# Stages of short products in a new order, mixing in 64x32 parts, and a new count of idle TensorE instructions

## The chip, the cores and the metric

The kernel runs on one core of a Trainium2 chip. The metric is device time in microseconds of one execution; the median of three runs is 1237.55 us (1237.3 to 1237.75). All arithmetic is in float32.

## What is computed

The input x has 128 sequences of 32 tokens with 512 channels. One layer does this (cut to what matters, norms and shapes in words):

```python
# x: (128, 32, 512); cond, adapter: one index per sequence
c = einsum('bct,bcd->bdt', x, cond_w[cond])          # mixing: a 32x32 matrix per sequence, over its tokens
q, k, v = split(clip(c @ w_qkv.T, -8, 8))            # projections; q and k then go through a layer norm
s = einsum('bqhd,bkhd->bhqk', q, k) / 4 + bias       # scores: 32 heads of 16, causal, ALiBi
x = x + einsum('bhqk,bkhd->bqhd', softmax(s), v) @ w_out.T      # weighted values, output projection
h = einsum('bsi,boi->bso', x, adapt_w[adapter])      # adapters: a 512x512 matrix per sequence
y = relu(h @ up_w) ** 2 @ down_w                     # shared part
y = y + (h @ fc1.T @ expert.T) * sum(top2(h @ gate_w)) @ fc2    # routed part, three matrices folded into one
out = x + layernorm(y)
```

## The kernel before

The 4096 tokens are cut into 32 tiles of 128 rows, so a tile is four sequences. Two tiles are a pair, whose shared part is computed together.

After a prologue for the first tiles, a loop runs over periods t = 2, 3, and so on. One period works on several tiles at once: weighted values, output projection and the turning of x for tile t; adapters for t-1; scores and softmax for t+1; mixing, q/k/v projections and the turning of q and k for t+2; routing for t-2; and half of the shared part of a pair. Even periods hold the up products (pu), odd ones the down products (pd), cut into eight parts `fill(0)` to `fill(7)` that stand between the other steps. TensorE's order is that of the program, with some orders fixed by hand: `after` orders two instructions without a wait on the chip, `wait` makes one wait for another. A planner in the framework orders the other engines' instructions by their dependencies and its own costs.

The order of TensorE in a period is: weighted values (`weigh`, psum po, L484), adapters (`adapt`, pad, L536), scores (`scores`, psc, L414), first half of the router (`route`, pr, L555), mixing (`mix`, pxc, L290), fill(0), two projections (`project`, pqkv, L307), output projection (`attend`, pw, L506), fills 1 to 3, third projection, second half of the router, fills 4 to 7.

A float32 product runs as two passes, each a weight load and a product. The full-size products use the whole array (128 rows x 128 columns). The adapters and weighted values use 128x32 parts of it, four side by side, each with its own 32 output rows; the scores use 64x32 parts, eight side by side, in two PSUM banks, one for each half of the rows. Mixing uses the whole array: its moving operand `blk` is a 128x128 matrix with the four sequences' 32x32 matrices on its diagonal (made by GpSimd in `blend`), its weights are the four 128-column parts of x. ScalarE copies the result to xcT (L295).

The scores' inputs are made late in the period before: q and k go to HBM and back to be turned (`swap`), ScalarE scales them (`scale`, L386 and L400), and VectorE spreads k over the heads (kx, L390). ScalarE's relu of the up products is L585.

`fill_up` puts idle instructions (`nc.tensor.nop`, L99) behind a fill: 7 in even periods, 71 in odd ones, 116 in period 2, spread over the eight fills. The next product that goes through `product` is ordered behind them.

`load_adapters` issues the next tile's adapter weights (4 MB) on SP's queue; in the loop its first transfer waits for the row maxima `mx` of tile t+1 (`cue`). PSUM has eight banks, handed out in turn.

Of the kernel before, what the change touches and what calls it, by code (L numbers as in the profile page):

```python
# [34 lines left out]
ROUT = (0, NE + D // 2, NE + D)  # L35


SHORT = (7, 71)
FIRST = 116
CLIP = 8.0  # L40
EPS = 1e-5
NEG = -1.0e30
# [3 lines left out]
def adaln_attn_ffn(  # L46
# [45 lines left out]


    queue = []

    def fill_up(n):

        for _ in range(n):
            nop = nc.tensor.nop("fill")  # L99
            after(nop, queue[-1])  # L100
            queue[:] = [nop]

    def product(*args, **kwargs):
        ins = nc.tensor.matmul(*args, **kwargs)  # L104
        if queue:
            after(ins, queue.pop())
        return ins


# [175 lines left out]
    def mix(t):  # L285

        s = tiles[t]
        pxc = bank(f"pxc_{t}")
        for c in range(DC):
            nc.tensor.matmul(  # L290
                pxc[:, ts(c, P)], lhsT=s["x"][:, ts(c, P)],
                rhs=s["blk"].rearrange("p a b -> p (a b)"), start=True, stop=True,
            )
        s["xcT"] = w2.tile([P, DC, P], F32, tag="xcT", name=f"xcT_{t}")
        nc.scalar.copy(s["xcT"].rearrange("p c n -> p (c n)"), pxc)  # L295

    def project(t, i, chunks=range(DC)):

        s = tiles[t]
        if chunks[0] == 0:  # L300
            if i == 0:
                s["qk"] = w2.tile([P, 2, D], F32, tag="qk", name=f"qk_{t}")
                s["v"] = w2.tile([P, D], F32, tag="v", name=f"v_{t}")
                s["mv"] = sm.tile([P, 2, 2], F32, tag="mv2", name=f"mv_{t}")
            s["pp", i] = bank(f"pqkv_{t}_{i}")
        for c in chunks:
            nc.tensor.matmul(  # L307
                s["pp", i], lhsT=s["xcT"][:, c, :], rhs=wqkv_sb[:, c, ts(i, D)],
                start=(c == 0), stop=(c == DC - 1),
            )  # L310
        if chunks[-1] < DC - 1:
            return
        nc.vector.tensor_scalar(  # L313
            out=s["qk"][:, i, :] if i < 2 else s["v"], in0=s["pp", i],
            scalar1=-CLIP, scalar2=CLIP, op0=ALU.max, op1=ALU.min,
        )
        if i < 2:
            st = sm.tile([P, 6], F32, tag="st", name=f"st_{t}_{i}")
            s["stats"] = nc.vector.bn_stats(out=st, in_=s["qk"][:, i, :])
            nc.vector.bn_aggr(out=s["mv"][:, i, :], in_=st)  # L320
# [13 lines left out]
                    after(add, done)  # L334

    last_flip = []
    last_pad = []

    def swap(srcs, name):

# [38 lines left out]
    def scale(t):  # L379

        s = tiles[t]
        q, k = s["T"][:, :, 0], s["T"][:, :, 1]

        s["kx"] = w1.tile([P, DC, SEQ, HQ, S], F32, tag="kx", name=f"kx_{t}")
        for c in range(DC):
            nc.scalar.activation(  # L386
                k[:, :, c], s["raw"][1][:, :, c], AF.Identity,
                bias=lnc[:, 3, c : c + 1], scale=lnc[:, 2, c : c + 1],
            )
            kx = nc.vector.tensor_tensor(  # L390
                out=s["kx"][:, c],
                in0=k[:, :, c].unsqueeze(2).broadcast_to([P, SEQ, HQ, S]),
                in1=m_half.unsqueeze(1).unsqueeze(3).broadcast_to([P, SEQ, HQ, S]),
                op=ALU.mult,
            )

            if c == 0 and last_flip:
                after(kx, last_flip[-1])
        for c in range(DC):
            nc.scalar.activation(  # L400
                q[:, :, c], s["raw"][0][:, :, c], AF.Identity,
                bias=qaff[:, 1, c : c + 1], scale=qaff[:, 0, c : c + 1],
            )

    def scores(t):

        s = tiles[t]
        s["s"] = w1.tile([P, H, S], F32, tag="s", name=f"s_{t}")
        banks = [bank(f"psc_{t}_{r}") for r in range(2)]
        for c in range(DC):  # L410
            for b in range(SEQ):
                for r in range(2):
                    rows_r = slice(r * P // 2, (r + 1) * P // 2)
                    psc = nc.tensor.matmul(  # L414
                        banks[r][ts(b, S), ts(c, HQ * S)],
                        lhsT=s["T"][rows_r, b, 0, c],
                        rhs=s["kx"][rows_r, c, b].rearrange("p h k -> p (h k)"),
                        start=True, stop=True,
                    )
                    if last_pad:  # L420
                        after(psc, last_pad.pop())
        s["psc"] = psc
        for r in range(2):
            add = nc.vector.tensor_tensor(
                out=s["s"].rearrange("p (c r h) k -> p r c (h k)", c=DC, r=2)[:, r],
                in0=banks[r].rearrange("p (c n) -> p c n", c=DC),
                in1=bias_sb.rearrange("p (c r n) -> p r c n", c=DC, r=2)[:, r],
                op=ALU.add,
            )
            s.setdefault("adds", []).append(add)  # L430
# [12 lines left out]
    def share(t):  # L443
        s = tiles[t]
        den = sm.tile([P, H], F32, tag="den", name=f"den_{t}")
        nc.vector.tensor_reduce(out=den, in_=s["s"], axis=AX.X, op=ALU.add)  # L446
        rden = sm.tile([P, H], F32, tag="rden", name=f"rden_{t}")
        nc.vector.reciprocal(rden, den)  # L448
        nc.gpsimd.tensor_tensor(  # L449
            out=s["s"], in0=s["s"], in1=rden.unsqueeze(2).broadcast_to([P, H, S]), op=ALU.mult  # L450
        )
# [28 lines left out]
    def weigh(t):  # L480
        s = tiles[t]
        po = bank(f"po_{t}")
        for h in range(H):
            nc.tensor.matmul(  # L484
                po[ts(h % 4, S), :].rearrange(
                    "p (e b i d) -> p e i b d", e=DC, b=SEQ, d=HD
                )[:, h // 8, h // 4 % 2],
                lhsT=s["pT"][:, h, :],
                rhs=s["vx"][h // (H // 2)][:, h % (H // 2)],
                start=True, stop=True,  # L490
            )


        s["aT"] = w1.tile([P, DC, SEQ, S], F32, tag="aT", name=f"aT_{t}")
        aT = nc.vector.transpose(
            out=s["aT"].rearrange("p e b q -> p (e b q)"), in_=po
        )
        if t == 0:
            after(tiles[2]["stats"], aT)

    def attend(t):

        s = tiles[t]
        pw = bank(f"pw_{t}")
        for g in range(4):
            nc.tensor.matmul(  # L506
                pw, lhsT=s["aT"][:, g].rearrange("p b q -> p (b q)"), rhs=wout_sb[:, g, :],
                start=(g == 0), stop=(g == 3),
            )
        nc.vector.tensor_tensor(out=s["x"], in0=s["x"], in1=pw, op=ALU.add)  # L510

    def turn_x(t):
# [9 lines left out]
    def adapt(t):  # L522
# [10 lines left out]
        for j in range(SEQ):  # L533
            for c in range(DC):
                for g in range(DC):
                    last_pad[:] = [nc.tensor.matmul(  # L536
                        pad[ts(g, S), ts(j, P)], lhsT=s["xT"][:, j, c],
                        rhs=s["adw"][c // 2][j][:, c % 2, ts(g, P)],
                        start=(c == 0), stop=(c == DC - 1),
                    )]  # L540
        nc.vector.transpose(
            out=pairs[t // GRP]["hT"][:, :, ts(t % GRP, P)].rearrange(
                "p e (j n) -> p e j n", j=SEQ
            ),
            in_=pad.rearrange("p (j e d) -> p e j d", j=SEQ, d=S),
        )

    def route(t, half):

# [25 lines left out]
    def up(g, f):  # L575
# [6 lines left out]
                start=(c == 0), stop=(c == DC - 1),  # L582
            )
        a = hp.tile([P, GRP * P], F32, tag="act", name=f"act_{g}_{f}")
        nc.scalar.activation(a, pu[:, : GRP * P], AF.Relu)  # L585
        nc.gpsimd.tensor_tensor(out=a, in0=a, in1=a, op=ALU.mult)  # L586
        pair["acts"].append(a)
        return last
# [186 lines left out]
    for t in range(GRP, NTILE + GRP):  # L775
# [2 lines left out]

        def fill(i):
            last = up(g, i) if t % GRP == 0 else down(g * GRP + i // 4, i % 4)  # L780
            short = FIRST if t == GRP else SHORT[t % GRP]
            queue[:] = [last]
            fill_up(short // 8 + (i < short % 8))

        when(here and t > GRP, weigh, t)
        when(t <= NTILE, adapt, t - 1)
        when(ahead, scores, t + 1)
        when(ahead, exponent, t + 1)
        if here:


            load_adapters(t, tiles[t + 1]["mx"] if ahead else None)
        if t == GRP:
            after(
                nc.sync.dma_start(out=gam_sb, in_=gamma.broadcast_to([P, D])),
# [2 lines left out]
        when(t + 3 < NTILE, load, t + 3)  # L798
        when(t > GRP and t % GRP == 0, finish, t - GRP - 1)
        when(t > GRP, route, t - GRP, 0)  # L800
        when(two, mix, t + 2)
        fill(0)
        when(two, project, t + 2, 0)
        when(ahead, share, t + 1)
        when(two, project, t + 2, 1)
        when(ahead, flip, t + 1)
        when(two, normalise, t + 2)
        when(two, turn, t + 2)
        when(here, attend, t)
        when(here, turn_x, t)  # L810
        fill(1)
        fill(2)
# [91 lines left out]
```

## Time and profile before

| | |
|---|---|
| median of three runs | 1237.55 us (1237.3 to 1237.75) |
| the profiled execution | 1237.27 us, span 1235.5 us |
| granted TensorE clock, mean | 0.999 |
| TensorE products (PE) | 1227.2 us busy, 99% |
| weight loads (PEld) | 790.5 us, 64% |
| VectorE, ScalarE, GpSimd | 658.3, 327.6, 431.5 us |
| one even and one odd period (from 607.06 us) | 37.77 and 37.69 us |

PE stands for the products of TensorE, PEld for its weight loads, PEldq for its sequencer's own instructions (semaphores, idle ones); DVE is VectorE, ACT ScalarE, POOL GpSimd, SP the engine that issues most transfers. A busy time is the union of the instructions' times; a product's recorded time holds its way through the array, so products overlap in the records, and a stage's length is read from the chain of waits, which cuts the time at each instruction's release. L414 is line 414 of the kernel before.

### The profile page before, as it was taken

The numbers are of one execution on the slowest core, as the hardware profiler recorded it, in microseconds if no ns is written. First come the engines' busy times: TensorE is split into PE (matmuls) and PEld (weight loads), VectorE is DVE, ScalarE is ACT, GpSimd is POOL, SyncE is SP. The second block draws the span as 40 slices with busy tenths as digits, with TensorE's granted clock in tenths as the row PEclk, the third lists the DMA queues.
The fourth block names the chain that finished last, engine by engine and source line by source line (L and its number), as shares of the span: only waits on it lengthen the run. The fifth ranks groups of instructions, "written<-read, shape, count | busy, mean of one in ns | idle before, by whom it ended". The sixth has DMA issues, their size and how long they took to land.

```text
span 1235.5 us, 29216 instructions
## 1 busy us (share of the span) xinstructions
PE 1227.2 (99%) x11614; PEld 790.5 (64%) x11614; DVE 658.3 (53%) x1090; ACT 327.6 (27%) x648; POOL 431.5 (35%) x393
## 2 busy tenths in 40 slices
PE   9999999999999999999999999999999999999998
PEld 4577466675666756567665666746667566675765
DVE  2975655646456464563646546465564645646222
ACT  2432223222222313133222232222322222231211
POOL 4543333433423424334243333333333242332410
PEclk9999999999999999999999999999999999999999
DMA  9745553435545345544355543455443554434630
GB/s 289 220 166 197 206 205 147 156 121 196 205 174 177 102 175 197 200 162 140 139 185 206 184 155 125 155 206 205 150 154 124 190 204 176 176 110 157 209 116 18
DMA packets 93417, 209.31 MB, mean 169 GB/s; under 512 B 11749, under 2 KB 42470, under 8 KB 93286
## 3 DMA queue, kind: packets, MB, share of 16 engines
q1 hardware_dynamic: 89142, 198.39, 45.8%
q0 software_dynamic: 3424, 8.39, 1.9%
q8 instruction: 97, 1.59, 0.5%
q10 hardware_dynamic: 720, 0.66, 0.2%
q14 instruction: 34, 0.28, 0.1%
HBM read 176.47 MB, written 30.93 MB: 168 GB/s over the span
## 4 chain that ended last, share of the span: by engine, by line
PE 99%; DMA 0%; DVE 0%; ACTq 0%; issue 0%; DVEq 0%
PE pqkv L307 27%; PE pu L104 18%; PE pd L104 17%; PE pr L555 10%; PE pad L536 9%; PE pw L506 9%; PE psc L414 3%; PE po L484 3%; PE pxc L290 2%; PE pro L207 1%; PE pd L636 1%; DMA fc_t<-in_fc_w 0%; PE pt L365 0%; PE pe L197 0%; PE pt_x L365 0%; ACTq L124 0%
## 5 line engine op out<-in xcount | busy, mean ns | idle before, releaser
L307 PE MATMUL pqkv<-wqkv_sb,xcT 128*128 128x512 f32 x768 | 340.3, 592 | 0.0
L307 PEld LDWEIGHTS pqkv<-wqkv_sb,xcT 128*128 128x128 f32 x768 | 145.5, 190 | 168.6 <-issue 162.8
L104 PE MATMUL pu<-hT,up_sb 128*128 128x256 f32 x1024 | 228.7, 379 | 0.0
L104 PE MATMUL pd<-down_sb,act 128*128 128x512 f32 x496 | 220.4, 592 | 0.0
L104 PEld LDWEIGHTS pu<-hT,up_sb 128*128 128x128 f32 x1024 | 193.5, 190 | 32.6 <-issue 6.9
L390 DVE TENSOR_TENSOR kx<-T_qk,m_half 128x512 f32<-128x512 f32 x128 | 110.4, 920 | 102.7 <-ACT T_qk L386 102.7
L104 PEld LDWEIGHTS pd<-down_sb,act 128*128 128x128 f32 x496 | 93.2, 190 | 104.7 <-issue 103.6
L471 POOL TENSOR_TENSOR vx<-v,msk 128x1024 f32<-128x1024 f32 x64 | 127.2, 2010 | 56.6 <-DVE v L313 49.9
L586 POOL TENSOR_TENSOR act<-act 128x256 f32<-128x256 f32 x128 | 77.9, 614 | 168.6 <-ACT act L585 168.6
L555 PE MATMUL pr<-rout_sb,hT 128*128 128x256 f32 (+1 forms) x512 | 125.8, 389 | 0.0
L536 PE MATMUL pad<-adw,T_x 128*32 128x128 f32 x4096 | 118.4, 273 | 0.1
L555 PEld LDWEIGHTS pr<-rout_sb,hT 128*128 128x128 f32 x512 | 94.7, 190 | 32.1 <-issue 19.9
L506 PE MATMUL pw<-wout_sb,aT 128*128 128x512 f32 x256 | 115.2, 592 | 0.0
L536 PEld LDWEIGHTS pad<-adw,T_x 128*32 128x32 f32 x4096 | 110.7, 110 | 2.0 <-issue 1.2
L436 POOL TENSOR_TENSOR s<-s,mx 128x1024 f32<-128x1024 f32 x32 | 61.7, 1928 | 143.4 <-DVE top L562 141.8
L446 DVE TENSOR_REDUCE den<-s 128x32 f32<-128x1024 f32 x32 | 39.0, 1220 | 100.5 <-ACT s L441 100.5
L520 POOL TENSOR_TENSOR x<-x,bet_sb 128x512 f32<-128x512 f32 x32 | 40.7, 1272 | 147.1 <-DVE blocks_x L346 144.8
L506 PEld LDWEIGHTS pw<-wout_sb,aT 128*128 128x128 f32 x256 | 48.6, 190 | 60.6 <-issue 60.0
L585 ACT ACTIVATE act<-pu 128x256 f32<-128x256 f32 x128 | 47.2, 379 | 139.6 <-PE pu L104 139.6
L623 POOL DMA_DIRECT2D out<-y x30 | 18.0, 599 | 179.8 <-DVE y L619 93.1
L449 POOL TENSOR_TENSOR s<-s,rden 128x1024 f32<-128x1024 f32 x32 | 61.4, 1919 | 51.2 <-DVE rden L448 48.3
L295 ACT COPY xcT<-pxc 128x512 f32<-128x512 f32 x32 | 18.8, 586 | 201.8 <-PE pxc L290 201.8
(76 smaller groups left out, 1094.5 us busy)
## 6 DMA issues: line engine op xcount, KB each, us to landing
adw<-in_adapt_w SPq DMA_DIRECT2D x256, 512.0 KB, 7.5
away_qk<-blocks_qk SPq DMA_DIRECT2D x28, 512.0 KB, 2.6
T_qk<-away_qk SPq DMA_DIRECT2D x112, 128.0 KB, 2.9
x<-in_x SPq DMA_DIRECT2D x32, 256.0 KB, 9.3
away_x<-blocks_x SPq DMA_DIRECT2D x30, 256.0 KB, 2.7
T_x<-away_x SPq DMA_DIRECT2D x120, 64.0 KB, 2.4
out<-y POOLq DMA_DIRECT2D x30, 256.0 KB, 2.7
wqkv_sb<-in_w_qkvT SPq DMA_DIRECT2D x12, 256.0 KB, 5.3
```

Of the source, the lines that this page charges most:

```text
L104: ins = nc.tensor.matmul(*args, **kwargs)
L307: nc.tensor.matmul(s["pp", i], lhsT=s["xcT"][:, c, :], rhs=wqkv_sb[:, c, ts(i, D)], start=(c == 0), stop=(c == DC - 1),)
L390: kx = nc.vector.tensor_tensor(out=s["kx"][:, c], in0=k[:, :, c].unsqueeze(2).broadcast_to([P, SEQ, HQ, S]), in1=m_half.unsqueeze(1).unsqu ...
L436: nc.gpsimd.tensor_tensor(out=s["s"], in0=s["s"], in1=mx.unsqueeze(2).broadcast_to([P, H, S]), op=ALU.subtract,)
L449: nc.gpsimd.tensor_tensor(out=s["s"], in0=s["s"], in1=rden.unsqueeze(2).broadcast_to([P, H, S]), op=ALU.mult)
L471: nc.gpsimd.tensor_tensor(out=vx, in0=s["v"][:, ts(half, D // 2)].rearrange("p (h d) -> p h d", d=HD).unsqueeze(2) .broadcast_to([P, H // ...
L506: nc.tensor.matmul(pw, lhsT=s["aT"][:, g].rearrange("p b q -> p (b q)"), rhs=wout_sb[:, g, :], start=(g == 0), stop=(g == 3),)
L520: nc.gpsimd.tensor_tensor(out=s["x"], in0=s["x"], in1=bet_sb, op=ALU.add)
L536: last_pad[:] = [nc.tensor.matmul(pad[ts(g, S), ts(j, P)], lhsT=s["xT"][:, j, c], rhs=s["adw"][c // 2][j][:, c % 2, ts(g, P)], start=(c == ...
L555: nc.tensor.matmul(pr[:, :n], lhsT=hT[:, c, ts(t % GRP, P)], rhs=rout_sb[:, c, ROUT[half] : ROUT[half + 1]], start=(c == 0), stop=(c == DC ...
L585: nc.scalar.activation(a, pu[:, : GRP * P], AF.Relu)
L586: nc.gpsimd.tensor_tensor(out=a, in0=a, in1=a, op=ALU.mult)
```

## The change

The order of TensorE in a period becomes scores (t+1), mixing (t+2), adapters (t-1), weighted values (t); in period 2 the adapters come first. The chain `short` fixes this order product by product.

Mixing of tiles 4 to 31 runs in 64x32 parts: 32 products of 64 columns, eight side by side (two row halves, each with two sequences, times four groups of 32 channels), into two PSUM banks; ScalarE copies them in two instructions. Tiles 0 to 3 keep the old form.

The idle instructions become 96 in even periods, 14 in odd ones and 5 in period 2, in seven groups: behind fills 0 to 3, behind each of the first two projections, and behind the output projection. The adapter weights' first transfer waits for the transpose behind the weighted values. ScalarE's relu of the fifth up part is ordered behind the scaling of q, and VectorE's sum of the exponentials behind the transpose of the weighted values.

```diff
-SHORT = (7, 71)
-FIRST = 116
+SHORT = (96, 14)
+FIRST = 5
...
+    def short(*args, **kwargs):
+
+        ins = product(*args, **kwargs)
+        if shorts:
+            after(ins, shorts[-1])
+        shorts[:] = [ins]
+        return ins
...
     def mix(t):
...
+        n = P // 2
+        banks = [bank(f"pxc_{t}_{r}").rearrange("p (c n) -> p c n", c=DC) for r in range(2)]
         for c in range(DC):
-            nc.tensor.matmul(
-                pxc[:, ts(c, P)], lhsT=s["x"][:, ts(c, P)],
-                rhs=s["blk"].rearrange("p a b -> p (a b)"), start=True, stop=True,
-            )
-        s["xcT"] = w2.tile([P, DC, P], F32, tag="xcT", name=f"xcT_{t}")
-        nc.scalar.copy(s["xcT"].rearrange("p c n -> p (c n)"), pxc)
+            for g in range(DC):
+                for r in range(2):
+                    short(
+                        banks[r][ts(g, S), c, :n],
+                        lhsT=s["x"][ts(r, n), c * P + g * S : c * P + (g + 1) * S],
+                        rhs=blk[ts(r, n), ts(r, n)], start=True, stop=True,
+                    )
+        for r in range(2):
+            nc.scalar.copy(s["xcT"][:, :, ts(r, n)], banks[r][:, :, :n])
...
-        nc.vector.tensor_reduce(out=den, in_=s["s"], axis=AX.X, op=ALU.add)
+        total = nc.vector.tensor_reduce(out=den, in_=s["s"], axis=AX.X, op=ALU.add)
+        if t > GRP:
+            after(total, last_head[-1])
...
+        relu = nc.scalar.activation(a, pu[:, : GRP * P], AF.Relu)
+
+        if f == FC // 2 and last_scale:
+            after(relu, last_scale.pop())
...
             queue[:] = [last]
-            fill_up(short // 8 + (i < short % 8))
+            if i < 4:
+                fill_up(i)
+
+        def fill_up(i):
+
+            if here:
+                lack = FIRST if t == GRP else SHORT[t % GRP]
+                idle_instructions(lack // 7 + (i < lack % 7))
 
-        when(here and t > GRP, weigh, t)
-        when(t <= NTILE, adapt, t - 1)
+        when(t == GRP, adapt, t - 1)
         when(ahead, scores, t + 1)
+        when(two, mix, t + 2)
+        when(GRP < t <= NTILE, adapt, t - 1)
+        when(here and t > GRP, weigh, t)
         when(ahead, exponent, t + 1)
...
-            load_adapters(t, tiles[t + 1]["mx"] if ahead else None)
+            load_adapters(t, last_head[-1])
...
         when(t > GRP, route, t - GRP, 0)
-        when(two, mix, t + 2)
         fill(0)
         when(two, project, t + 2, 0)
+        fill_up(4)
         when(ahead, share, t + 1)
         when(two, project, t + 2, 1)
+        fill_up(5)
...
         when(here, attend, t)
+        fill_up(6)
```

## The prediction

> **What bounds the kernel now.** First the page: the busy times, the chain that ended last and the DMA queues.
>
> ```profile
> PE 1227.2 (99%) x11614; PEld 790.5 (64%) x11614; DVE 658.3 (53%) x1090; ACT 327.6 (27%) x648; POOL 431.5 (35%) x393
> ...
> PE 99%; DMA 0%; DVE 0%; ACTq 0%; issue 0%; DVEq 0%
> ...
> q8 instruction: 97, 1.59, 0.5%
> ```
>
> TensorE never waits, so the time is the sum of its stages, and only a shorter stage or a new wait can move it. The last line counts the instruction code: the trace has 24,843 TensorE records (11,614 loads, as many products, 1,322 idle ones, some 290 semaphores), over 97 packets 256 each.
>
> Then the chain of waits around one even period (start us, us, what):
>
> ```profile
> 607.13 1.03 PE po L484 x64
> 608.16 3.51 PE pad L536 x128
> 611.67 1.08 PE psc L414 x64
> 612.75 1.98 PE pr L555 x8
> 614.73 0.89 PE pxc L290 x8
> 615.62 1.73 PE pu L104 x8
> 617.35 6.87 PE pqkv L307 x16
> ```
>
> The last line gives the array's pace: 6.87 us for 16 passes of 512 columns, 0.84 ns a column. By it weighted values (po: 16 rounds of four concurrent 64-column products) need 0.86, adapters (pad: 32 rounds, 128 columns) 3.44, scores (psc: 8 rounds of eight, 128 columns) 0.86, router (pr: 8 x 264) 1.77, mixing (pxc: 8 x 128) 0.86. What is over is 0.17, 0.07, 0.22, 0.21 and 0.03: about 0.2 us wherever the array shape changes (three times), nearly nothing elsewhere.
>
> Third, how fast instructions arrive: weight loads in narrow windows of the scores (611.60 to 611.68, 612.02 to 612.14), then idle instructions of one odd period, then the timeline of an early period (scores at 68.92).
>
> ```profile
> L414 PEld LDWEIGHTS psc<-kx,T_qk x16: 103/104/106, 611.6 to 611.7; 64*32 64x32 f32 x16
> L414 PEld LDWEIGHTS psc<-kx,T_qk x14: 102/104/107, 612.0 to 612.1; 64*32 64x32 f32 x14
> L99 PEldq NOP  x71: 13/13/13, 651.0 to 675.6; - x71
> 68.92 1.35 PE L414 MATMUL psc<-kx,T_qk 64*32 64x128 f32 x64
> 70.20 1.12 PE L307 MATMUL pqkv<-wqkv_sb,xcT 128*128 128x512 f32 x2
> ```
>
> Queued pairs of load and product start 5 ns apart; once the queue has run dry, 14 take 0.12 us, 8.4 ns a pair. The sequencer runs some 16 pairs ahead: it takes the adapters' first semaphore at 607.75, when 48 of the 64 weighted values have started, and the second 0.11 us later; idle instructions in a row are 0.07 apart. The early scores took 1.28 us to the next stage, not 1.08: their loads stop for 0.2 us some 64 instructions ahead of the count's fifth block of 256. So short products can become bound by supply.
>
> **The change part by part.** *Order.* Scores, mixing, adapters, weighted values run through the shapes 64x32, 64x32, 128x32, 128x32, then 128x128: still three changes, 0.60 us. No gain from the order alone, if all inputs are there.
>
> *Mixing.* Tiles 4 to 31, 28 periods. 8 passes of 128 columns become 64 of 64 columns, eight at once (two row halves, four column groups): 8 rounds x 64 x 0.84 ns = 0.43 us at the array's pace, 0.54 (64 x 8.4 ns) at that of supply. Mixing follows 64 pairs of scores, which already run the queue dry, so I take 0.54. It begins with a wait (POOL's mask), after which the scores show an 0.08 us hole: 0.10. The adapters' two semaphores lay under the weighted values and now follow a dry queue: 0.22, half under the shape change, so 0.11. The scores' 0.22 over holds 0.10 of late supply, which the 0.54 counts again. Mixing thus costs 0.54 + 0.10 + 0.11 - 0.10 = 0.65. Bounds: 0.43, with a filled queue and no waits, and 1.39, with the early scores' 1.28 in the place of 0.54. I take the value near the lower end because every scores stage of the 28 periods ran at 8.4 ns once dry. Mixing takes two PSUM banks instead of one from the ring of eight; eight allocations back stand the projections of the period before, long read.
>
> Five stages after: changes 0.60, scores 0.86, mixing 0.65, adapters 3.49, weighted values 0.86, router 1.77 = 8.23, against 1.03 + 3.51 + 1.08 + 1.98 + 0.89 = 8.49: **0.26 saved**.
>
> The Trainium skill ("TensorE: Matmul & The Clock Gate", Part 1, "Wait — 56ns, not 53.3ns?") says that products never start less than about 25 ns apart, however short. By that page this mixing would take 1.6 us and the change be an estimated 20 us slower; the 64 weighted values above, in 1.03 us, go against it, and no number here rests on it.
>
> *Seven blocks.* A product counts four instructions (two passes, a load each). An even period now has 128 for weighted values, 256 adapters, 128 scores, 32 router, 16 mixing, 128 up, 48 and 16 for the projections, which is 752, with 7 idle ones and 9 semaphores 768, exactly three blocks; an odd one (64 down, 71 idle) too. Counted in the trace, every one starts 173 into a block. Mixing adds 112 to each. Even: 752 + 112 + 96 idle + 9 semaphores = 969; odd: 688 + 112 + 14 + 9 = 823; together 1792, seven blocks. Period 2 has 111 idle instructions fewer and 112 more products, period 3 57 fewer and 112 more, so from tile 4 an even period starts 229 into a block. Its second boundary comes 283 after its start, just inside the adapters, and 64 ahead of that is the middle of mixing: there I put the 0.2 us hole. An odd period starts at 174; its holes fall at 18 (queue full) and 274 (adapters, slow): covered. Saved: 0.06 in even, 0.26 in odd periods, 0.16 on average. Fetches: packets at 610.08 and 613.56 took 1.1 us, and by my stage times no two of the new boundaries are passed less than 2.5 us apart; nothing. A fetch that came late would add its lateness to each pair of periods.
>
> *Idle instructions.* 14 in a row are 14 x 0.07 = 1.0 us of sequencer. They follow full-size products, and 16 pairs ahead are 16 x 0.21 = 3.4 us or more; the 71 and 116 of before cost no gap either. Nothing; uncovered, 1 us a group.
>
> *Scores first, 4.5 us earlier.* They need the spread keys and scaled queries, made late in the period before. DVE of an odd period, the next weighted values, then ACT and DVE of an even period:
>
> ```profile
> 601.19 4.20 DVE L390 TENSOR_TENSOR kx<-T_qk,m_half 128x512 f32<-128x512 f32 x4 [1.92 <-ACT T_qk L386]
> 607.06 1.10 PE L484 MATMUL po<-vx,pT 128*32 128x64 f32 x64
> 641.48 0.38 ACT L585 ACTIVATE act<-pu 128x256 f32<-128x256 f32 x1 [1.34 <-PE pu L104]
> 641.76 1.64 ACT L386 ACTIVATE T_qk<-T_qk,lnc 128x128 f32<-128x128 f32 x4
> 642.28 2.63 DVE L390 TENSOR_TENSOR kx<-T_qk,m_half 128x512 f32<-128x512 f32 x4 [5.28 <-ACT T_qk L386]
> ```
>
> Odd: ready at 605.39, 1.7 us before the period ends. Even: 644.91, when it ends at 644.83; ACT put two activations first. The new rule puts the fifth one behind the query scaling, so the work starts about 3 us earlier, as in odd periods. Cost nothing, with 1.7 us of cover; behind a wait would stand all of TensorE. Mixing, 7 us earlier, needs its x (issued at 620.84, landing 9.3 later) and the mask (POOL, 617.36): of the period before, over 10 us of cover.
>
> *Queues.* Adapter weights are issued on SP after the weighted values' transpose instead of the row maxima (615.46 now), by my stage sums about a microsecond earlier, with x and the swaps behind them; they are read some 30 us later. The sum of the exponentials, now ordered behind that transpose, waits for ScalarE until 619.02 anyway. Row maxima, sums, and two ACT copies instead of one (0.38 each by the 256-column row above) have 6 us and more before the projections. The router waits longest for the hidden tile's transpose: two stages lie between. Nothing.
>
> Sum: 28 x 0.16 = 4.5 us. The profiled execution took 1237.27 (span 1235.5), 0.28 below the median of 1237.55: 1233.0 on the median's footing.
>
> **The rivals.** *Array pace:* the queue stays filled and no hole falls in mixing; 0.43 and no extra waits, 0.48 saved, 13 us: 1224. For it: po runs 64 pairs without a hole. Against: the scores' 8.4 ns.
>
> *A wash:* more waits in mixing and holes in both kinds of period take all: about 1237.
>
> *Supply gives out (slower):* mixing runs as the early scores did. 1.39 is 0.74 over the 0.65, so 0.74 - 0.26 = 0.48 is lost a period: 28 x 0.48 = 13 us, 1251. It decides above 0.91 us for mixing with its waits (0.65 + 0.26), which is 12.5 ns a pair. For it: that row; against: every later scores stage took 1.08.
>
> *Keys late:* each microsecond beyond the 1.7 costs up to 28 us; half a microsecond gives 1233 + 14 = 1247. For it: the planner's order of DVE and ACT can shift. Against: the same margins in every period.
>
> **How the numbers follow.** Forecast 0.52 (1229 to 1236), array pace 0.15, wash 0.13, supply 0.13, keys 0.07. The range 1224 to 1243 leaves out the last two beyond small sizes and a little below. About 0.2% (2.5 us) can be told from no change: faster 0.51 + 0.14 = 0.65, same 0.15, slower 0.20.
>
> **What would show it.** Periods of about 37.6 and 37.4 us instead of 37.77 and 37.69; 64 pxc in 0.5 to 0.8 us behind psc; no row of TensorE waiting for DVE or ACT. Wrong, if pxc takes over 0.9 us, if the scores wait for keys, or if the sum of the other stages moves.

## The result, and the profile after

The changed kernel takes 1242.38 us (median of 7 runs, 1241.06 to 1242.96) against 1237.46 us for the kernel before in the same session (7 runs, 1236.73 to 1237.86): ratio 1.0039, 95% interval 1.0027 to 1.0050. It is slower by 0.4%, where 1233.0 was forecast. The profiled execution took 1242.96 us with a span of 1240.9, against 1237.27 and 1235.5 before, so the two profiles hold the whole difference (and 0.8 us more: the profiled execution of after is the slowest of its seven).

The page of after, the lines that answer to those shown of before (busy times, chain that ended last, the queue of TensorE's instruction code):

```profile
PE 1230.0 (99%) x13182; PEld 792.2 (64%) x13182; DVE 685.8 (55%) x1090; ACT 330.6 (27%) x676; POOL 462.9 (37%) x393
...
PE 99%; issue 0%; DVE 0%; DVEq 0%
...
q8 instruction: 110, 1.80, 0.6%
```

TensorE is still the whole chain, with 1,568 products more (28 x 56) and 13 blocks of code more; the page alone does not say why it is slower. The chain of waits around one even and one odd period does (start us, us, what; "issue" is time in which TensorE waited for nothing that the profile shows):

```profile
611.94 1.04 PE psc L105 x62
612.98 0.69 PE pxc L105 x46
613.67 2.52 PE pad L105 x83
616.19 0.02 issue
616.21 1.40 PE pad L105 x42
...
649.90 1.04 PE psc L105 x62
650.94 0.69 PE pxc L105 x46
651.63 1.88 PE pad L105 x64
653.52 0.18 issue
653.70 1.96 PE pad L105 x62
655.66 0.93 PE po L105 x63
656.60 1.98 PE pr L585 x8
```

Scores 1.04 (1.08 before), mixing 0.69 (0.89; forecast 0.65), weighted values 0.93 (1.03), router 1.98 as before: together about where the forecast put them. But the adapters took 3.51 and now take 3.94 and 4.02, and there is a break in each. The weight loads show it plainly (timeline of TensorE's loads, odd and even period; the bracket is the idle time before the row):

```profile
652.90 0.44 PEld L105 LDWEIGHTS pad<-adw,T_x 128*32 128x32 f32 x13
653.72 0.39 PEld L105 LDWEIGHTS pad<-adw,T_x 128*32 128x32 f32 x14 [0.38 <-issue]
...
616.23 0.36 PEld L105 LDWEIGHTS pad<-adw,T_x 128*32 128x32 f32 x13 [0.28 <-issue]
```

From the start of one load to the next 0.49 us pass in odd periods and 0.40 in even ones, where loads otherwise follow each other by 0.027 on average. No semaphore stands at that place in the program: among the adapters only the first product waits. As far as the profile shows, TensorE had no instruction. What GpSimd did in the meantime, in the same two periods of after, and in the same even period of before:

```profile
613.78 0.88 POOL L287 TENSOR_TENSOR blk<-cw,msk 128x128 f32<-128x128 f32 x1 [5.34 <-PE pxc L105]
614.93 1.01 POOL L238 DMA_INDIRECT cw<-in_cond_w,rows  x1 [0.27 <-POOL blk L287]
616.93 2.35 POOL L461 TENSOR_TENSOR s<-s,mx 128x1024 f32<-128x1024 f32 x1 [0.99 <-DVE mx L460]
...
651.74 0.40 POOL L287 TENSOR_TENSOR blk<-cw,msk 128x128 f32<-128x128 f32 x1 [0.73 <-PE pxc L105]
652.42 1.01 POOL L238 DMA_INDIRECT cw<-in_cond_w,rows  x1 [0.27 <-POOL blk L287]
```

```profile
615.49 1.90 POOL L436 TENSOR_TENSOR s<-s,mx 128x1024 f32<-128x1024 f32 x1 [3.42 <-DVE top L562]
617.36 0.39 POOL L278 TENSOR_TENSOR blk<-cw,msk 128x128 f32<-128x128 f32 x1
618.02 1.04 POOL L229 DMA_INDIRECT cw<-in_cond_w,rows  x1 [0.27 <-POOL blk L278]
```

Before, GpSimd's mask and the row gather behind it followed the softmax's subtraction and ran under products of 512 columns. The mask waits for a buffer that the mixing frees ("<-PE pxc"). Before, the mixing ended at 615.62, just behind the start of the subtraction (615.49), and the planner had the mask follow the subtraction. Now the mixing ends at 613.67, 3.3 us ahead of the subtraction's start, and the planner has put mask and gather ahead of the subtraction: they fall into the adapters. Both stops end 0.29 us after the gather does (615.94 and 616.23, 653.43 and 653.72), while the table load of ScalarE beside them ends 0.45 us ahead of the stop's end in even periods and 0.12 in odd ones, and the last block of code had landed at differing times (0.0 to 5.2 us ahead of the stop's end).

Compared event by event (start of each tile's output projection), after loses 2.6 us up to the fourth, then 0.18 to 0.20 us in nearly every one of the next 20 periods (4.0 in all), and from period 25 to 29 gains 0.10 to 0.26 a period. The sign changes where the gathers end: the rows of tile 31 are fetched in period 23. In periods 25 to 29 the adapters take 3.63 to 3.70 us, without a break like those, and the periods 37.46 to 37.66 against 37.70 and 37.76 before.

### The profile page after: what moved, and what is told of

Its sections match the earlier page's. It is cut to its first block, busy times and chain, and to the rows that moved or that the text cites. A ratio compares the mean times of both kernels' runs of the same rounds, so it can differ in the third digit from the quotient of the medians.

```text
span 1240.9 us, 32583 instructions
## 1 busy us (share of the span) xinstructions
PE 1230.0 (99%) x13182; PEld 792.2 (64%) x13182; DVE 685.8 (55%) x1090; ACT 330.6 (27%) x676; POOL 462.9 (37%) x393
## 4 chain that ended last, share of the span: by engine, by line
PE 99%; issue 0%; DVE 0%; DVEq 0%
PE pqkv L105 27%; PE pu L105 18%; PE pd L105 17%; PE pad L105 10%; PE pr L585 10%; PE pw L105 9%; PE psc L105 3%; PE po L105 2%; PE pxc L105 2%; PE pro L216 1%; PE pd L669 1%; PE pe L206 0%; PE pt L392 0%; PE pxc L302 0%; PE pi L177 0%
## 5 line engine op out<-in xcount | busy, mean ns | idle before, releaser
L417 DVE TENSOR_TENSOR kx<-T_qk,m_half 128x512 f32<-128x512 f32 x128 | 139.0, 1145 | 55.0 <-ACT T_qk L413 55.0
L619 POOL TENSOR_TENSOR act<-act 128x256 f32<-128x256 f32 x128 | 90.1, 712 | 177.4 <-ACT act L615 177.4
L498 POOL TENSOR_TENSOR vx<-v,msk 128x1024 f32<-128x1024 f32 x64 | 134.7, 2129 | 56.7 <-DVE v L339 50.0
L105 PE MATMUL pad<-adw,T_x 128*32 128x128 f32 x4096 | 126.0, 274 | 2.9 <-issue 2.2
L339 DVE TENSOR_SCALAR qk<-pqkv 128x512 f32<-128x512 f32 x64 | 44.1, 689 | 80.2 <-PE pqkv L105 80.0
L461 POOL TENSOR_TENSOR s<-s,mx 128x1024 f32<-128x1024 f32 x32 | 67.8, 2120 | 41.9 <-DVE mx L460 41.7
L484 DVE STREAM_TRANSPOSE pT<-s 128x1024 f32<-128x1024 f32 x32 | 39.8, 1244 | 61.1 <-POOL s L476 61.1
L225 ACT ACTIVATE std_f<-mvf,eps 128x1 f32<-128x1 f32 x32 | 9.4, 295 | 218.2 <-DVE mvf L642 211.0
```

The source lines that it names most:

```text
L339: nc.vector.tensor_scalar(out=s["qk"][:, i, :] if i < 2 else s["v"], in0=s["pp", i], scalar1=-CLIP, scalar2=CLIP, op0=ALU.max, op1=ALU.min,)
L417: kx = nc.vector.tensor_tensor(out=s["kx"][:, c], in0=k[:, :, c].unsqueeze(2).broadcast_to([P, SEQ, HQ, S]), in1=m_half.unsqueeze(1).unsqu ...
L461: nc.gpsimd.tensor_tensor(out=s["s"], in0=s["s"], in1=mx.unsqueeze(2).broadcast_to([P, H, S]), op=ALU.subtract,)
L484: pT = nc.vector.transpose(out=s["pT"].rearrange("p h q -> p (h q)"), in_=s["s"].rearrange("p h k -> p (h k)"),)
L498: nc.gpsimd.tensor_tensor(out=vx, in0=s["v"][:, ts(half, D // 2)].rearrange("p (h d) -> p h d", d=HD).unsqueeze(2) .broadcast_to([P, H // ...
```

## The experiments

Each kernel was compared with the kernel before on the same chip (1237.2 to 1237.9 in the six sessions). "Stop" is a gap of over 0.17 us between two weight loads of one short stage. Two kinds matter here: a stop that ends 0.1 to 0.35 us behind a gather, and one that ends 1.2 to 1.6 us behind the landing of a block of code.

### The gather

**Late gather.** GpSimd's mask and gather go behind the subtraction again; TensorE's order is that of the change.

```
+        if t - 7 > GRP:
+            after(gather, subs[t - 7])
...
+        if t - 3 > GRP:
+            after(mask, subs[t - 3])
```

> The changed kernel, with GpSimd's mask and row gather ordered behind the softmax's subtraction again, as they stood in the kernel before; TensorE's order is untouched. Theory (the gather): in the changed kernel the adapters stop for 0.49 us in odd and 0.40 us in even periods, and each stop ends 0.29 us after the end of the row gather that the earlier mixing has let forward into the adapters. Moved, the gather lies in the 512-column products of even periods and at the end of the weighted values in odd ones; the stops go, periods 4 to 23 become some 0.45 us shorter each, 20 x 0.45 = 9 us in all: 1233.5, between 1232.5 and 1235. Rival (ScalarE's function table load, which runs in the same microsecond): the stops stay where they are, 1242.4. Rival (the instruction fetch): the stops stay, 1242.4.

Measured: 1235.47 us, ratio to before 0.9988 (0.9979 to 0.9997): 6.9 us less than the changed kernel, and now a little faster than before. Its chain and its GpSimd, an odd period:

```profile
646.22 3.63 PE pad L105 x128
649.85 0.10 PE po L105 x5
649.95 0.06 issue
650.01 1.08 PE po L105 x59
```

```profile
648.30 1.91 POOL L467 TENSOR_TENSOR s<-s,mx 128x1024 f32<-128x1024 f32 x1 [2.71 <-DVE mx L466]
...
650.84 1.01 POOL L240 DMA_INDIRECT cw<-in_cond_w,rows  x1 [0.27 <-POOL blk L291]
```

The adapters' stop is gone. 2 of the expected 9 us are missing: a smaller stop shows in some periods, here at the start of the weighted values, in even periods late in the adapters, and it is of the other kind (below).

**Early gather in the kernel before.** The opposite edit: TensorE unchanged, mask and gather wait for the weighted values' transpose.

```
+            wait(ins, cue)      # gather of tile t + 7; cue: transpose of po
...
+            wait(mask, cue)
```

> The kernel before, with nothing changed on TensorE, but GpSimd's mask and row gather brought forward into the adapters (they wait for the transpose of the weighted values instead of following the subtraction; the gather fetches the rows of the same tile four periods ahead, for tiles up to 31). Theory (the gather): a stop of 0.4 to 0.5 us appears in the adapters of each period that gathers, some 21 of them: 1237.5 + 9 = 1246.5, between 1244 and 1248. Rivals (table load, instruction fetch, the order of TensorE's stages): no stop, 1237.5.

Measured: 1246.93 us, ratio 1.0075 (1.0061 to 1.0089), 9.4 us more, as expected. Its chain and GpSimd in an even period:

```profile
614.20 3.04 PE pad L557 x107
617.24 0.05 issue
```

```profile
615.99 1.16 POOL L225 DMA_INDIRECT cw<-in_cond_w,rows  x1 [0.27 <-POOL blk L289]
```

The stop of 0.42 us is there with the old order of stages and old blocks of code: it came with mask and gather. Code cannot be what is waited for here: in this period the last block had landed at 609.72, 7.56 us ahead of the stop's end (617.28). In even periods the stop ends 0.13 us after the gather, in odd ones 0.29 as in the changed kernel.

**Plain transfer.** In the changed kernel, with the gather replaced:

```
+            nc.gpsimd.dma_start(out=cw, in_=cond_w[ts(t % 4, P), :])
```

> The changed kernel with a plain transfer of the same size on GpSimd's queue in the place of the row gather, for tiles 7 and up (it fetches fixed rows, so it leaves out the choice by index). Theory (it is the gather by index that takes TensorE's instructions away; GpSimd's plain transfers of the output lie beside the scores in the kernel before and cost nothing there): the stops go, 1234, between 1233 and 1236. Rival (any transfer that GpSimd starts does it): the stops stay, 1242.4.

Measured: 1236.76 us, ratio 0.9990 (0.9981 to 1.0000); no stop at that place, though GpSimd's mask and ScalarE's table load stayed where they were. So neither of these two makes it by itself. An odd period:

```profile
643.89 1.04 PE psc L105 x62
644.93 0.69 PE pxc L105 x46
645.62 3.63 PE pad L105 x128
649.25 0.89 PE po L105 x64
650.15 1.98 PE pr L588 x8
```

A stop of this kind shows behind gathers by index alone, but whether the choice by index itself is needed is not shown: the kernels below lose the stop with the gather left in place.

**Two gathers.** A second one straight behind the first (`after(gather, first)`).

> The changed kernel with a second row gather straight behind the first, of the same rows into memory that nothing reads, for tiles 7 and up. Theory (TensorE gets no instructions for about 0.9 us in each gather and stands for what its queue does not cover): a second stop of 0.4 to 0.5 us in the adapters, 1.3 us behind the first, in some 20 periods: 1242.4 + 9 = 1251.5, between 1249 and 1254. Rival (what stops TensorE is GpSimd's mask or the table load of ScalarE beside it): one stop as before, 1242.4.

Measured: 1236.73 us, ratio 0.9994 (0.9985 to 1.0004). A miss for both: not two stops behind gathers, but none (those at blocks of code stay). The first gather begins 1.3 us behind the start of the adapters, as in the changed kernel:

```profile
608.89 3.63 PE pad L105 x128
```

```profile
610.14 1.01 POOL L240 DMA_INDIRECT cw<-in_cond_w,rows  x1 [0.27 <-POOL blk L293]
611.46 0.95 POOL L240 DMA_INDIRECT chan<-in_cond_w,rows  x1 [0.30 <-issue]
```

So a gather at that place is not enough. Five more kernels asked what else it takes.

**One and six multiplications behind.** In the place of the second gather, 1 or 6 small multiplications (`nc.gpsimd.tensor_tensor(out=spare, in0=ident[:, :S], ...)`).

> The changed kernel with one small multiplication on GpSimd (128x32, into memory that nothing reads) between the row gather and the softmax's subtraction, for tiles 7 and up. Theory A (TensorE is stopped when GpSimd, behind a gather by index, comes to an instruction that must wait; in the changed kernel the subtraction waits there for VectorE's maximum): the next instruction is ready, as it was with two gathers, so the stops go, 1236.5, or only those of even periods stay (there the wait outlasts the small multiplication), 1240. Theory B (two gathers did it by where the descriptors of the gather come to lie): nothing changes, 1242.4.

> As the kernel with one multiplication behind the gather, with six, of which four stand between the gather and the subtraction: about as long as the wait. Theory A: no stop in even or odd periods, 1236.5. Theory B: the stops stay, 1242.4.

Measured: 1243.32 us (ratio 1.0045, 1.0030 to 1.0060) and 1243.19 us (1.0048, 1.0033 to 1.0064). All stops stayed, 0.4 to 0.6 us, also where the subtraction followed the multiplications without a wait: theory A falls.

**One more transfer elsewhere.** Behind the softmax's multiplication, 9 us from the gather, one plain transfer or one gather more per period:

```
+            after(nc.gpsimd.dma_start(out=spare, in_=cond_w[0:P, :]), scaled)
```

> The changed kernel with one more plain transfer on GpSimd's queue per period (128x32, into memory that nothing reads), behind the softmax's multiplication and so far from the adapters; the row gather stays where the change has it. Theory C (what counts is how the transfers of GpSimd's queue follow one another: in the changed kernel every gather reuses the completion semaphore of the gather four periods back, with a transfer more it does not): the stops in the adapters go, 1236.5. Theory D (what counts is a second gather straight behind the first): the stops stay, 1242.4.

> As the kernel with one more plain transfer, with a gather by index in that place. Theory C: the stops in the adapters go, 1236.5. Theory D: they stay, and the second gather, under products of 512 columns, costs nothing itself: 1242.4.

Measured: 1236.62 us (0.9994, 0.9984 to 1.0003) and 1236.32 us (0.9991, 0.9982 to 1.0001): no stop follows a gather in either, with the gather itself where the change put it (plain transfer elsewhere, an even period; adapters 609.21 to 612.87):

```profile
610.46 1.04 POOL L239 DMA_INDIRECT cw<-in_cond_w,rows  x1 [0.27 <-POOL blk L288]
...
619.56 0.58 POOL L481 DMA_DIRECT2D chan<-in_cond_w  x1
```

**Rows touched early.** The transfers as in the change; only GpSimd's wait for the rows' landing is moved away from the mask.

```
+            nc.gpsimd.tensor_tensor(out=spare[:, :1], in0=cw[:, :1], in1=cw[:, :1], op=ALU.mult)
```

> The changed kernel with one small multiplication on GpSimd (128x1) that reads the gathered rows soon after they land, for tiles 5 and up, so that GpSimd's wait for their landing stands there and no longer straight ahead of the mask four periods later; the transfers, their order and their completion semaphores are those of the changed kernel. Theory E (the wait ahead of the mask is part of what stops TensorE): the stops go, 1236.5. Theory F (it is the succession of the transfers: every gather takes the completion semaphore of the gather four periods back): the stops stay, 1242.4.

Measured: 1246.47 us, ratio 1.0067 (1.0050 to 1.0083). All stops stayed (0.49 to 0.52 and 0.43 to 0.46); of the 4 us more than in the changed kernel 2.5 were lost ahead of the first output projection, where the scores of tile 0 had three breaks of 0.5 to 0.7 us. Theory E falls. Of the ten kernels with a transfer of the rows in the adapters, the six with a stop behind nearly every one share a gather by index and a queue in which gather and output alternate, so that each gather takes the completion semaphore of the gather four periods back; the four without lack one or the other. But this does not hold gather by gather. In the changed kernel the stop of period 3 (0.51 us) follows a gather ahead of which only gathers had gone through the queue, and "tile 4 whole" (below) has such a stop though its outputs and gathers go two by two. Nor is it the semaphore alone: before and with the late gather, too, each gather takes that of the gather four periods back, and with one more transfer elsewhere the gathers of periods 3 to 5 took one that a gather had used last, and no stop followed. So theory F is not shown, and what takes TensorE's instructions away stays open.

### The blocks of instructions

**Half a block off.** `FIRST = 133` in the place of 5.

> The changed kernel with 128 more idle instructions in its first period only, so that all later stages lie half a block of 256 instructions further on. Theory (supply by blocks: a block is asked for when the one before is entered, and is there 3.4 us later): the bounds now fall at instructions 90, 346 and 602 of the short stages in even periods and at 141, 397 and 653 in odd ones, and the 256 instructions between them take 2.1, 2.85 and 2.55 us, so TensorE stands some 1.3 + 0.55 us in even periods and 0.85 us in odd ones; part of it covers the stop after the gather. 14 pairs x 2.7 less up to 9: between 1265 and 1280. Rival (blocks are fetched well ahead, the alignment is worth nothing): 1242.4.

Measured: 1270.58 us, ratio 1.0272 (1.0258 to 1.0286), as expected. An even period of it:

```profile
623.38 1.43 PE pad L105 x42
624.81 0.95 issue
625.76 2.45 PE pad L105 x81
...
628.92 0.86 issue
```

Both stops stand where the shifted bounds fall, 1.0 to 1.3 and 0.6 to 1.1 us long in most even periods; in odd ones one of 0.2 to 1.25 us stands at the 70th product of the adapters. The 3.4 us of the theory had come from the changed kernel's first period: TensorE resumes at 87.33, the next packet (one brings a block) starts at 88.37 and lands at 89.37, TensorE resumes at 90.70, 256 instructions later. So where the bounds of the blocks fall is worth 28 us here (1270.58 against 1242.38).

**Tile 4 whole.** `if t < 2 * GRP + 1:` in `mix`, and `FIRST = 117`.

> The kernel with the late gather, with tile 4's mixing alone left in eight whole products (its instructions are replaced by idle ones in the first period, so later stages keep their place). It asks what the first period of the main loop lost: there TensorE stood 0.70 us in the adapters and 1.23 us in the mixing, each time until 1.36 us after a block of instructions had landed. Theory (supply by blocks): the second stop goes with the 112 instructions, and the whole products cost 0.24 us more than the parts: 1.0 us less than the kernel with the late gather, 1232.5 if that takes 1233.5. Rival (the early loss comes from a wait for data in the new order): the same as the kernel with the late gather, or 0.2 us more.

Measured: 1236.98 us, ratio 0.9999 (0.9990 to 1.0008): 1.5 us more than with the late gather, not 1.0 less. The stop in the mixing did go, but one period later three breaks of 0.66, 0.39 and 0.66 us came in the weighted values, the last at 124.99, 0.28 us behind the end of a gather that ran a little earlier there (123.72 to 124.71). The rival, a wait for data, shows in no row of the profile.

**Bounds 14 later.** `SHORT = (110, 0)` with the late gather.

> The kernel with the late gather, with the 14 idle instructions of odd periods moved into even ones (110 and 0), so that in even periods alone the bounds of the blocks fall 14 instructions later in the short stages. Theory (supply by blocks): the bound moves from the 106th to the 113th product of the adapters, 7 x 0.027 = 0.19 us later, while the block is asked for only some 0.08 us later; the stops of even periods shrink by about 0.1 us, 13 x 0.1: 1234.2. Rival (the stop belongs to what runs beside the adapters, not to the count): it stays at the 106th product, 1235.5.

Measured: 1235.65 us, ratio 0.9988 (0.9979 to 0.9997). The stop of even periods moved from the 106th to the 113th product, so it belongs to the count; but where it stood it was longer (0.29 to 0.62 against mostly 0.19), and nothing was gained. That goes against the 3.4 us as a fixed time: with more time between the bounds the stop should have shrunk.

**Prologue shifted.** Eight groups of 21 idle instructions behind projections ahead of the main loop, `FIRST = 93`.

> The late gather and the bounds 14 later (1235.65), with eight times 21 idle instructions behind long products ahead of the main loop and correspondingly many in its first period, so that later periods keep their place. Supply by blocks: in the scores of tile 2 (0.2 to 0.5 us) and in the mixing of tile 4 (0.6 to 0.9 us) TensorE stands for a block of instructions; 168 instructions earlier the bounds fall under longer work, all but 0.25 us of it goes: 1234.6. Rival (these stops only move to another place of the first periods): 1235.65 or more.

Measured: 1236.02 us, ratio 0.9986 (0.9977 to 0.9995). Both stops of the first periods went (1.1 us), but the idle instructions cost as much ahead of the first output projection (1.05 us): nothing gained.

**Equal phases.** Both kinds of period four blocks long, so that both meet the bounds alike; with the gather as in the late gather, and behind the multiplication.

```
-SHORT = (96, 14)
+SHORT = (147, 219)
...
+            fill_up(7)          # and behind the fifth and sixth fill
```

> The kernel with the late gather, and idle instructions of 147 in even and 219 in odd periods (ten parts a period) in the place of 96 and 14, so that each period is four blocks of 256 and every period's short stages meet the block bounds at the same places: just ahead of the scores, at the start of the adapters and at their end. The kernel with the late gather (1235.5) still stands 0.19 to 0.51 us at the 106th product of the adapters in some even periods and 0.32 to 0.40 us at the 6th product of the weighted values in some odd ones, each time until 1.3 to 1.5 us after a block landed; its shortest periods are 37.44 and 37.50 us, and periods 4 to 29 are 5.2 us over that in all. Theory (supply by blocks decides what is left): most of the 5.2 us goes, 1230.5, between 1229 and 1232.5. Rival (the idle instructions, 22 in a row at 0.07 us against products of 1.7 us, let the queue run dry): 1235 to 1240.

> As the kernel with equal phases, with the mask and the row gather behind the softmax's multiplication, so that in odd periods too the gather falls under the products of 512 columns and not under the router. Theory (a gather costs nothing where TensorE's queue holds longer work than the 0.9 us for which it gets no instructions): the same as the kernel with equal phases, at most 0.3 us less, 1230.5. Rival (each gather costs TensorE its time wherever it stands): the same as well in total, but stops of 0.4 us would show in the products behind it.

Measured: 1264.23 us (1.0212, 1.0191 to 1.0233) and 1262.64 us (1.0208, 1.0194 to 1.0222). A miss by 34. All odd periods but one took 37.50 to 37.60 us, nearly without stops, as hoped, but most even ones stood in the adapters:

```profile
619.00 0.45 PE pad L106 x9
619.44 1.43 issue
```

**Bounds ahead.** `THIRD = 233` (the idle instructions of the second period) to bring the bound ahead of the scores; again with both places of the gather.

> The kernel with equal phases, with 26 idle instructions more in the second period alone, which brings the bounds of the blocks from the 20th instruction of the scores to some 6 ahead of them, in all later periods. With equal phases as they were, the even periods stood 1.7 to 2.0 us at the 10th product of the adapters: the block there was asked for only some 0.3 us into the scores, so that 256 instructions passed in 1.9 us. Theory (a block is asked for when the one before is entered, and costs nothing if 256 instructions take 3.4 us or more): asked for ahead of the scores, the next at the start of the adapters, the third at their end, all stops of both periods go, 1230.5, between 1229 and 1233. Rival (the many idle instructions late in a period hold the sequencer up): the stops of even periods stay, 1255 or more.

> As the kernel with the bounds ahead, with the mask and the row gather behind the softmax's multiplication, away from the router of odd periods. Theory: the same as that kernel or up to 0.5 us less, since its odd gathers end less than 1 us behind the weighted values: 1230.3.

Measured: 1264.26 us (1.0231, 1.0212 to 1.0250) and 1269.12 us (1.0259, 1.0245 to 1.0273): a miss again. The stop moved with the bound, to the 62nd product of the mixing, and stayed 1.8 to 2.4 us long:

```profile
541.12 0.66 PE pxc L106 x44
541.78 1.85 issue
543.63 0.30 PE pxc L106 x3
```

In this period the block's packet started at 541.06, 1.05 us into the scores; in an even period without a stop (scores at 618.25) it had started at 614.17, 4.1 us ahead of them. Why the block is mostly asked for so late in even periods, which come out of products of 512 columns, the runs do not show. In the two profiles five of these stops, 2.1 to 2.2 us long, cost more than themselves: within 0.7 us of their end TensorE's granted clock fell to 0.5 for 3.4 us (from 1006.1 to 1009.5, where the adapters took 5.30 us, not 3.63). In the other profiles it stays at 1.0 throughout the main loop.

### The parts

**Mixing whole.** The new order of stages with the late gather, mixing in eight whole products in all tiles, idle instructions 3 and 75.

> As the kernel with equal phases, with all mixing in eight whole products (six blocks for a pair of periods, 3 and 75 idle instructions): the new order of stages without the parts. Theory (array and shape changes): whole mixing takes 0.89 us against 0.69 in parts, and the order then has one more change of the array's shape, 0.2 us: 28 x 0.4 = 11 us more than the kernel with equal phases, 1241.5, between 1239 and 1243. Rival (the parts save nothing, since what they spare the array the supply takes): the same as the kernel with equal phases, 1230.5.

Measured: 1250.38 us, ratio 1.0103 (1.0088 to 1.0119). The size was meant against equal phases, which failed; the periods without a stop answer it: 37.88 and 37.94 us, against 37.44 and 37.50 for the late gather's. The parts are worth 0.44 us a period, and the new order without them would be 0.18 worse than before (37.70 and 37.76). The chain of one odd period:

```profile
654.22 1.09 PE psc L106 x64
655.30 1.09 PE pxc L309 x8
```

Whole products cost 1.09 between the two kinds of short stage, 0.69 in parts, and the scores 0.05 more.

## Why the prediction was wrong

*The five stages: right.* Forecast 8.23 us against 8.49, 0.26 less a period. The odd period with a plain transfer shows it without a stop: 1.04 + 0.69 + 3.63 + 0.89 + 1.98 = 8.23. Without stops the late gather's periods are 37.44 and 37.50 us, 0.26 less than before in both kinds. Mixing measured 0.69 for 0.65; its 64 products start 11 ns apart. The 25 ns between starts of the Trainium skill's page "TensorE: Matmul & The Clock Gate" (Part 1, "Wait — 56ns, not 53.3ns?") thus do not bound products on different parts of the array. 28 x 0.26 would have been 7.3 us.

*"Queues ... Nothing": the step that failed.* It went through adapter weights, row maxima, sums and copies, and the mask came in only as something that mixing needs ("over 10 us of cover", under "Scores first"). It did not ask the reverse: what mixing, once earlier, lets go. The mask was waiting for it, the gather is queued behind the mask, and the two went ahead of the subtraction into the stretch of shortest products, where TensorE stops 0.49 and 0.40 us behind the gather. 20 periods x 0.445 us are 8.9 us, and a gain of 5.2 in those periods (20 x 0.26) turned into a loss of 4.0. Late and early gather show it from both sides, -6.9 and +9.4 us. The profile before could not show such a stop: there the gather ran under long products.

*"Seven blocks": hole in the wrong place, threshold too low.* 0.2 us were put into the mixing of every even period, 0.10 a period on average, 2.8 us in all. From period 3 on no stop shows in the mixing. The count was followed only to the second bound of the short stages, and the stops stand at the third, 256 instructions on (by the same count at 475 in even and 530 in odd periods): even periods stand late in the adapters (9 of 13 with the late gather, 0.18 to 0.51) and some odd ones at the start of the weighted values (5 of 13, 0.32 to 0.40): 4.2 us of stops in periods 4 to 29. In the changed kernel the stop after the gather mostly covered them. That "no two of the new boundaries are passed less than 2.5 us apart; nothing" was a mis-sized term: a block takes about 3.4 us, and in even periods the 256 instructions up to the 106th adapter product take about 3.2 (from 1.4 to 4.6 us behind the start of the scores).

*The first periods: not costed.* The sum began with tile 4. In the profiled run of after, 2.6 us were lost by the fourth output projection, most of them in stops of 0.70 and 1.23 us for blocks of code; in that of the late gather 0.9. So 7.3 us gained, 8.9 and 2.6 lost: 4.2 slower, of the 4.9 between the medians; the rest stays unassigned.

*The rivals.* "Supply gives out" had the right resource but the wrong place and price: it was to decide above 0.91 us for mixing, which took 0.69; TensorE ran out of instructions in the adapters. That 1242.4 lies inside the stated range (1224 to 1243) is luck: no rival had the gather in it. "Keys late" did not come: the last keys of the odd and the even period are ready 1.7 and 1.3 us ahead of the scores (611.87 and 649.83):

```profile
606.00 4.20 DVE L417 TENSOR_TENSOR kx<-T_qk,m_half 128x512 f32<-128x512 f32 x4 [1.92 <-ACT T_qk L413]
643.92 4.61 DVE L417 TENSOR_TENSOR kx<-T_qk,m_half 128x512 f32<-128x512 f32 x4 [1.92 <-ACT T_qk L413]
```

Idle instructions in the first parts cost nothing, as said: the stages behind them take 6.87, 3.43 and 5.18 us as before.

*Its own test held.* "Wrong, if the sum of the other stages moves": the adapters moved, and looking there led to the cause.

## What to carry to other kernels

When a step is moved earlier, list what waits for it on every engine, and what is queued behind that, DMAs included: the released work is moved too, and it may land where TensorE's queue is thinnest. Count a run of short products in instructions as well as in time: here 256 of them in less than some 3.4 us mostly made TensorE stand. Two order edges on an engine that is off the critical path were worth 6.9 us here, nearly the 7.3 that the change itself was to bring.

## What the runs showed of the hardware that was not expected

- A row gather by index on GpSimd (1.0 us) could stop TensorE's instructions with no semaphore between them: 0.49 us in odd and 0.40 in even periods, the end 0.29 us behind the gather's in the changed kernel. If TensorE's queue of some 16 pairs, at 0.027 us a pair, covers another 0.4, an estimate of the whole is 0.9 us. The rows themselves move only later (packets from 654.13 to 654.55, the stop ended at 653.72). The Trainium skill says ("Perfetto Trace Analysis", "DMA Instruction — SWDGE (GPSIMD)") that such an instruction's row in a profile ends when the last descriptor is written, not when data have moved; these times agree. So the stop lies beside the end of the gather's row and just behind it, not beside the transfer; by that page this is the writing of descriptors.
- One more transfer per period in GpSimd's queue, plain or by index, straight behind the gather or 9 us away, took these stops away altogether (1236.3 to 1236.7 us for 1242.4). Alternating transfers and completion semaphores go with the stops over ten kernels, but not gather by gather; the mechanism is open.
- TensorE's code comes in blocks of 256 instructions, in the changed kernel's first period 3.4 us apart: 1.0 from resuming to the packet's start, 1.0 for the packet, 1.3 until the first instruction runs (1.2 to 1.6 in the other stops of this kind). Half a block of idle instructions in the wrong place cost 28 us.
